# One layer of a four-layer network: a hand-written issue order by slots, with the neighbouring images' stages as pieces in it

## Chip, cores, metric

The kernel runs on one core of one Trainium2 chip. The metric is the device time of one execution in microseconds: the median of the runs, and beside it one profiled execution whose trace all durations come from.

## What is computed

Four layers, each `x = x + layer(group_norm(x))`, on `x` of shape (4 images, 64, 64, 128), all in float32. The change touches layer 0 only, a two-dimensional selective scan:

```python
xz = x @ in_proj_w.T
xh, z = jnp.split(xz, 2, axis=-1)          # 256 channels each
z = jax.nn.silu(z)
xc = silu(depthwise_conv3x3(xh) + conv_b)  # per image 256 x 64 x 64
x0 = xc.reshape(B, 256, L)                 # L = 4096, row by row
x1 = transpose(xc, (0, 1, 3, 2)).reshape(B, 256, L)
xs = stack([x0, x1, x0[..., ::-1], x1[..., ::-1]], axis=1)   # 4 directions
dts, Bm, Cm = split(einsum('bkdl,kcd->bkcl', xs, x_proj_weight), [8, 24], 2)
delta = softplus(einsum('bkrl,kdr->bkdl', dts, dt_projs_weight) + bias)
h[t] = exp(delta[t] * A) * h[t-1] + delta[t] * u[t] * B[t]   # 16 states a channel
y[t] = sum over states of h[t] * C[t]
y = ((y0 + y2[::-1] + transpose(y1 + y3[::-1]) + D * xs) - mean) / sqrt(var + eps)
out = (y * out_norm_w + out_norm_b) * z @ out_proj_w.T
```

## The kernel before

Layer 0 (`layer0`, line 86) runs over the four images one after the other (line 136). Line numbers are those of the listing at the end of this section. For one image:

- **Stage before the scan** (lines 138 to 186). Eight loads of x (`xt`, 512 tokens each), transposes to channels by tokens (line 65), group statistics, one scaling of `xn`. For each half `s` of the 256 channels: the projection `xh` (157), copied into a padded image (158), and the 3x3 convolution as nine matmuls with diagonal weights (163), through Silu into `xc` (170), which stays in SBUF. The gate `z` goes to DRAM (186).
- **Scan** (lines 209 to 306). The image's 4096 tokens are cut in 8 chunks of 512; four directions `k`, in the order 1, 3, 0, 2, give 32 *units* (k, c). `view4` reads `xc` in the direction's order by strides. For each unit `inputs` (189) makes `xd` (the 40 rows of time step, B and C), stores the B rows to DRAM (`bd`), makes `delta` by Softplus and `du = delta * u`. The 16 states go in 4 groups `g` of 4 (`q`). For each state: GpSimd multiplies `dB = du * Bb` (242), where `Bb` is loaded from DRAM to all partitions, ScalarE makes `dA = exp(delta * A)` (245) in PSUM for each half, VectorE runs the scan into `h` (246). In this text one state, so one dB, two dA and two scans, is a *slot*; a unit has 16.
- **Product with C** (lines 253 to 285). For each group `cr` spreads C over partitions (254) and `W` masks it (256). Then for each quarter of the chunk and each half-quarter `e`: four transposes of `h` into PSUM (`pt`, 269), one copy to SBUF (`hT`, 271), and the products `yT` (277), each into 32 of the 128 partitions. A float32 matmul is two records in the trace, a transpose is one.
- **Sum over directions** (287 to 306): `yT` plus what the earlier directions left in DRAM (`yr`), stored again; for k = 2 the layer-norm statistics.
- **Stage after the scan** (309 to 340): normalise, multiply by two broadcast rows and z on GpSimd (322 to 324), transpose (329), output projection (336), add x, store.

Nothing in the file orders this by hand. The framework sorts the instructions of every engine, SyncE's DMA queue included, by its own priorities and places the waits; each engine then runs its list in order. Buffers bound how far engines run apart: `dA`, `pt` and the shared tag `m` (projections, `cr`, convolution) have two PSUM banks each, `dB` and `Bb` three buffers, `h` two, shared with the padded image.

The listing shows the functions touched and their callers.

Of the kernel before, what the change touches and what calls it, by code (L numbers as in the profile page):

```python
# [15 lines left out]
P = 128  # L16
NB = 4
# [7 lines left out]


def view4(t, k, c):

    v = t.rearrange("p s (h w) -> p s h w", w=64)
    if k % 2:  # L30
        v = t.rearrange("p s (h w) -> p s w h", w=64)
    if k < 2:
        return v[:, :, 8 * c : 8 * c + 8, :]
    return v[:, :, 56 - 8 * c : 64 - 8 * c, :][:, :, ::-1, ::-1]


class Shared:
# [19 lines left out]
    def group_norm(self, src, psum, small, keep=None, tag="gt"):  # L57
# [4 lines left out]
        for c in range(NCH):  # L62
# [4 lines left out]
            if keep is not None:  # L67
                nc.scalar.copy(keep[:, c * CH : (c + 1) * CH], ps)
        mv = small.tile([P, 2], F32, name="gn_mv")
# [16 lines left out]
def layer0(sh, A, x_in, x_out, scr):  # L86

    tc, nc = sh.tc, sh.nc  # L90
    with ExitStack() as ctx:
        pool = lambda name, bufs, **kw: ctx.enter_context(tc.tile_pool(name=name, bufs=bufs, **kw))
        wp = pool("l0w", 1)
        big = pool("l0big", 1)
        tmp = pool("l0tmp", 2)
        small = pool("l0small", 2)
        io = pool("l0io", 3)
# [5 lines left out]
        cols = wp.tile([P, 36], F32, name="cols")  # L103
# [5 lines left out]
        on_rows = wp.tile([P, 2, 2 * P], F32, name="on_rows")  # L109
        nc.sync.dma_start(on_rows, A["l0_rows"].partition_broadcast(P))  # L110
# [23 lines left out]
        tiles4 = lambda ap: ap.rearrange("(q p) d -> p q d", p=P)  # L134

        for b in range(NB):

            xn = big.tile([P, NT], F32, name="xn")
            xt = []
            for c in range(NCH):  # L140
                t = io.tile([P, 4, DM], F32, name="xt")
                nc.sync.dma_start(t, tiles4(x_in(b)[c * CH : (c + 1) * CH, :]))
                xt.append(t)
            s_, o_ = sh.group_norm(lambda j: xt[j // 4][:, j % 4, :], ps, small, keep=xn, tag="m")
            nc.vector.tensor_scalar(xn, xn, s_, o_, ALU.mult, ALU.add)


            xc = big.tile([P, 2, NT], F32, name="xc")
            for s in range(2):
                pad = big.tile([P, 66, 66], F32, name="pad", tag="h", bufs=2)  # L150
                nc.gpsimd.memset(pad[:, 0, :], 0.0)
                nc.gpsimd.memset(pad[:, 65, :], 0.0)
                nc.gpsimd.memset(pad[:, 1:65, 0], 0.0)
                nc.gpsimd.memset(pad[:, 1:65, 65], 0.0)
                for c in range(NCH):
                    pm = ps.tile([P, CH], F32, name="xh", tag="m")
                    nc.tensor.matmul(pm, lhsT=w_in[:, s, :], rhs=xn[:, c * CH : (c + 1) * CH], start=True, stop=True)
                    nc.scalar.copy(pad[:, 1 + 8 * c : 9 + 8 * c, 1:65], pm.rearrange("p (h w) -> p h w", w=64))
                for c in range(NCH):
                    pm = ps.tile([P, CH], F32, name="cv", tag="m")  # L160
                    for t in range(9):
# [4 lines left out]
                            rhs=pad[:, 8 * c + dy : 8 * c + dy + 8, dx : dx + 64],  # L166
# [3 lines left out]
                    nc.scalar.activation(xc[:, s, c * CH : (c + 1) * CH], pm, AF.Silu, bias=conv_b[:, s : s + 1])  # L170

            for c in range(NCH):
                z = tmp.tile([P, 4, 2 * P], F32, name="z")
                for e in range(2):
                    zp = ps.tile([P, 2, 2 * P], F32, name="zp", tag="m")
                    for q in range(2):
                        t0 = c * CH + (2 * e + q) * P
                        nc.tensor.matmul(
                            zp[:, q, :],
                            lhsT=xn[:, t0 : t0 + P],  # L180
                            rhs=w_in[:, 2:4, :].rearrange("p s d -> p (s d)"),
                            start=True,
                            stop=True,
                        )
# [987 lines left out]
```

## Time and profile before

| | us |
|---|---|
| median of 3 runs | 10997.95 (10985.44 to 11008.58) |
| profiled execution: its own time | 10996.99 |
| profiled execution: span, first to last instruction | 10995.2 |
| busy TensorE / VectorE / ScalarE / GpSimd | 9042.7 / 7870.9 / 6496.6 / 5549.4 |
| last store's sum of layer 0 (`xr`, line 339) | 7817.6 |
| scans of image 0 / 1 / 2 / 3, first unit's start | 200.7 / 2151.3 / 4102.2 / 6057.9 |

A span is shorter than the execution's time by what lies ahead of the first and behind the last instruction. Busy time of TensorE is modelled from its instructions' size and contains waiting in the pipeline; where it matters, starts are compared instead. The granted clock is TensorE's share of full speed. The idle time at the end of a group's line is that of its engine just before the group's instructions, with what ended most of it.

### The profile page before, as it was taken

The numbers are of one execution on the slowest core, as the hardware profiler recorded it, in microseconds if no ns is written. First come the engines' busy times: TensorE is split into PE (matmuls) and PEld (weight loads), VectorE is DVE, ScalarE is ACT, GpSimd is POOL, SyncE is SP. The second block draws the span as 40 slices with busy tenths as digits, with TensorE's granted clock in tenths as the row PEclk, the third lists the DMA queues.
The fourth block names the chain that finished last, engine by engine and source line by source line (L and its number), as shares of the span: only waits on it lengthen the run. The fifth ranks groups of instructions, "written<-read, shape, count | busy, mean of one in ns | idle before, by whom it ended". The sixth has DMA issues, their size and how long they took to land.

```text
span 10995.2 us, 136237 instructions
## 1 busy us (share of the span) xinstructions
PE 9042.7 (82%) x48616; PEld 4817.3 (44%) x48616; DVE 7870.9 (72%) x11236; ACT 6496.6 (59%) x11794; POOL 5549.4 (50%) x3106
## 2 busy tenths in 40 slices
PE   8888887888888888888887888888797666576777
PEld 4433444443344344334444333444575334344555
DVE  2788887277888717788881778888445876877777
ACT  3778876377888727778871778887222102114555
POOL 2777877277788727778872777887200000000000
PEclk9999999889999988999998899999898667678999
DMA  2223322222233222223322222332300011010000
GB/s 71 86 98 105 108 101 92 74 86 94 101 110 106 86 79 87 95 99 110 105 91 69 97 95 102 107 108 95 106 16 22 20 31 31 0 31 7 9 9 9
DMA packets 375737, 811.01 MB, mean 74 GB/s; under 512 B 24546, under 2 KB 289506, under 8 KB 309266
## 3 DMA queue, kind: packets, MB, share of 16 engines
q1 hardware_dynamic: 372946, 799.82, 21.7%
q8 instruction: 385, 6.31, 0.2%
q14 instruction: 294, 2.41, 0.1%
q10 hardware_dynamic: 2112, 2.48, 0.1%
HBM read 680.58 MB, written 121.63 MB: 73 GB/s over the span
## 4 chain that ended last, share of the span: by engine, by line
PE 61%; DVE 21%; ACT 10%; issue 4%; DMA 2%; POOL 2%; ACTq 0%; DVEq 0%; SPq 0%; POOLq 0%
PE yT L277 15%; PE pt L269 14%; DVE h L246 10%; ACT hT L271 6%; PE cr L254 5%; PE cv L163 5%; PE pm L776 2%; PE xd_ps L193 2%; PE po L923 2%; ACT dA L245 2%; PE dp L201 2%; PE ps L891 1%; DVE W L256 1%; PE po L441 1%; PE pf L436 1%
## 5 line engine op out<-in xcount | busy, mean ns | idle before, releaser
L246 DVE TENSOR_TENSOR_SCAN h<-dA,state,dB 128x512 f32<-128x512 f32 x4096 | 5016.9, 1271 | 1398.9 <-POOL dB L242 699.8
L242 POOL TENSOR_TENSOR dB<-du,Bb 128x1024 f32<-128x1024 f32 x2048 | 4842.1, 2370 | 1267.6 <-DVE h L246 1006.4
L245 ACT ACTIVATE dA<-delta,A_neg 128x512 f32<-128x512 f32 x4096 | 2788.5, 696 | 527.8 <-DVE h L246 514.3
L269 PE MATMUL pt<-ident,h 128*128 128x128 f32 x16384 | 2667.0, 292 | 348.4 <-DVE h L246 348.1
L269 PEld LDWEIGHTS pt<-ident,h 128*128 128x128 f32 x16384 | 1838.6, 145 | 2000.1 <-issue 1280.2
L271 ACT COPY hT<-pt 128x512 f32<-128x512 f32 x4096 | 2252.5, 587 | 748.9 <-PE pt L269 737.8
L277 PE MATMUL yT<-hT,W 128*32 128x256 f32 x16384 | 2324.7, 403 | 355.5 <-ACT hT L271 353.2
L277 PEld LDWEIGHTS yT<-hT,W 128*32 128x32 f32 x16384 | 540.0, 109 | 1440.3 <-ACT hT L271 1019.9
L696 POOL COPY XG<-Xs 64x1 f32<-64x1 f32 x4 | 0.7, 180 | 1784.9 <-ACT Xs L667 1784.9
L204 POOL TENSOR_TENSOR du<-delta,xc 128x1024 f32<-128x1024 f32 x128 | 335.0, 2617 | 763.2 <-ACT delta L202 763.2
L254 PE MATMUL cr<-xd,sel 40*128 40x512 f32 x1024 | 624.6, 715 | 49.4 <-ACT delta L202 36.3
L256 DVE TENSOR_TENSOR W<-cr,diag 128x512 f32<-128x512 f32 x512 | 351.1, 686 | 395.4 <-PE cr L254 264.1
L163 PE MATMUL cv<-pad,taps 128*128 128x512 f32 x1152 | 496.2, 592 | 0.0
L883 POOL COPY vw<-pad 128x196 f32<-128x196 f32 x256 | 76.5, 350 | 702.6 <-PE pv L915 590.7
L193 PE MATMUL xd_ps<-xc,w_x 128*40 128x512 f32 x512 | 354.3, 817 | 93.4 <-DVE W L256 91.1
L776 PE MATMUL pm<-PT,Xs 64*128 64x512 f32 x512 | 380.3, 919 | 16.3 <-DVE pr L777 16.3
L163 PEld LDWEIGHTS cv<-pad,taps 128*128 128x128 f32 x1152 | 216.9, 189 | 278.0 <-issue 274.4
L170 ACT ACTIVATE xc<-cv,cols 128x512 f32<-128x512 f32 x64 | 44.0, 687 | 446.6 <-PE cv L163 446.6
L923 PE MATMUL po<-PT,V 98*128 98x256 f32 x1024 | 278.4, 394 | 35.6 <-DVE PT L919 35.6
L628 ACT COPY S<-pa 128x512 f32<-128x512 f32 x96 | 56.2, 585 | 420.6 <-PE pa L621 420.6
L201 PE MATMUL dp<-xd,w_dt 8*128 8x512 f32 x512 | 291.4, 653 | 6.1 <-ACT xd L195 6.1
L581 PE MATMUL in_pm<-in_mv,tok 128*128 128x32 f32 x48 | 14.1, 386 | 324.4 <-DVE in_mv L579 324.4
(268 smaller groups left out, 9455.2 us busy)
## 6 DMA issues: line engine op xcount, KB each, us to landing
Bb<-l_B SPq DMA_DIRECT2D x512, 1024.0 KB, 4.7
l_y<-y SPq DMA_DIRECT2D x128, 512.0 KB, 3.1
yr<-l_y SPq DMA_DIRECT2D x64, 512.0 KB, 4.8
l_z<-z SPq DMA_DIRECT2D x32, 512.0 KB, 2.9
zf<-l_z SPq DMA_DIRECT2D x32, 512.0 KB, 3.9
yr<-l_y SPq DMA_DIRECT2D x64, 256.0 KB, 4.9
yf<-l_y SPq DMA_DIRECT2D x32, 512.0 KB, 4.7
xt<-in_x SPq DMA_DIRECT2D x32, 256.0 KB, 3.0
```

Source lines behind the costliest of these rows:

```text
L163: nc.tensor.matmul(pm, lhsT=taps[:, s, t, :], rhs=pad[:, 8 * c + dy : 8 * c + dy + 8, dx : dx + 64], start=(t == 0), stop=(t == 8),)
L193: nc.tensor.matmul(xd_ps, lhsT=w_x[:, s, k, :], rhs=u[:, s], start=(s == 0), stop=(s == 1))
L201: nc.tensor.matmul(dp, lhsT=w_dt[:, k, s * P : (s + 1) * P], rhs=xd[0:8, :], start=True, stop=True)
L242: nc.gpsimd.tensor_tensor(dB, du, Bb[:, q : q + 1, :].to_broadcast([P, 2, CH]), ALU.mult)
L245: nc.scalar.activation(dA, delta[:, s, :], AF.Exp, scale=A_neg[:, k, s, n : n + 1])
L246: nc.vector.tensor_tensor_scan(h[:, s, :, q], dA, dB[:, s, :], state[:, s, n : n + 1], ALU.mult, ALU.add)
L254: nc.tensor.matmul(cr, lhsT=sel[:, g, :], rhs=xd, start=True, stop=True)
L269: nc.tensor.transpose(pt[:, r, s, :], h[:, s, t0 : t0 + 32, :].rearrange("p t n -> p (t n)"), sh.ident)
L271: nc.scalar.copy(hT, pt.rearrange("p r s d -> p r (s d)"))
L277: nc.tensor.matmul(yT[e][32 * jo : 32 * jo + 32, qo % 2, :], lhsT=W[:, 4 * q + j, :], rhs=hTs[j // 2][:, j % 2, :], start=((e, jo) not in ...
L776: nc.tensor.matmul(pm, lhsT=Xs[:, r, :], rhs=PT[:, 8 * g : 8 * g + 8, :], start=True, stop=True)
L923: nc.tensor.matmul(po[:, e], lhsT=V[:, half, :], rhs=PT[:, half].rearrange("p h q -> p (h q)"), start=(half == 0), stop=(half == 1),)
```

## The change

The new `layer0` writes the order of TensorE, ScalarE, VectorE and GpSimd itself: everything in the `manual_schedule` block is issued on these four in the order of the program text. SyncE is not in that list and is still ordered by the framework.

- All 128 units of the four images form one loop, 16 slots each. A slot issues dB, its two exp and scan pairs, then one call of `transposed`: the eight transposes and two copies of one quarter of the *oldest finished group*, and behind them the four products of the quarter transposed *one slot earlier*. `h` and `W` have three buffers.
- `cr` comes in every slot with q = 1, `W` with q = 2, the state copies with q = 2 of the next group (the last one in slot 1 of the next unit). The next unit's `inputs` are cut in five and issued in slots 7, 8, 9, 10 and 13; its `u` is fetched in slot 3.
- The stage before the scan is a generator `before(b)`, the stage after it `after(b)`. Image b+1's `before` and image b-1's `after` run beside image b's scan, one piece at most in a slot, in slots 0 to 6 and 13 to 15 if the piece has room (a convolution block needs ten slots in a row, one tap each). What is left at an image's end is issued at once. `before(0)` runs ahead of the block, the last `after` behind the last unit.
- `xc` is no longer kept in SBUF. Each convolution output goes through Silu twice, row by row (`xo`) and transposed (`xw`), and both are stored to DRAM; `fetch` loads a unit's 512 columns from one of them. The stores of `xw` write runs of 8 floats. x is loaded and transposed twice in `before`, once for the statistics and once per chunk with its two neighbouring rows for the convolution (a row projected in two chunks where they overlap).
- The two row products of the layer norm on GpSimd become scale and bias of the copy that follows the transposes on ScalarE. `z` is kept by channels. The D term's products move from direction 2 to direction 0. The sum over directions is added in place in `y`.

The diff, cut to the added lines that matter; the removed ones are in the listing above.

```diff
+        def before(b):
...
+                t = tmp.tile([P, 6, DM], F32, name="xt", bufs=1)
+                nc.sync.dma_start(t[:, 0 : j1 - j0], tiles(x_in(b)[j0 * P : j1 * P, :]))
...
+                for s in range(2):
+                    yield 10
                     pm = ps.tile([P, CH], F32, name="cv", tag="m")
                     for t in range(9):
...
+                        if t < 8:
+                            yield 1
+                    zp = ps.tile([P, CH], F32, name="zp", tag="m")
+                    nc.tensor.matmul(zp, lhsT=w_in[:, 2 + s, :], rhs=xn[:, o : o + CH], start=True, stop=True)
+                    xo = tmp.tile([P, CH], F32, name="xo", tag="t2", bufs=4)
+                    nc.scalar.activation(xo, pm, AF.Silu, bias=conv_b[:, s : s + 1])
+                    nc.sync.dma_start(scr(f"xr{b % 2}")[s, :, c * CH : (c + 1) * CH], xo)
+                    xw = tmp.tile([P, 64, 8], F32, name="xw", tag="t2", bufs=4)
+                    nc.scalar.activation(
+                        xw, pm.rearrange("p (h w) -> p w h", w=64), AF.Silu, bias=conv_b[:, s : s + 1]
+                    )
+                    nc.sync.dma_start(scr(f"xw{b % 2}")[s].rearrange("p (w h) -> p w h", h=64)[:, :, 8 * c : 8 * c + 8], xw)
+                    z = tmp.tile([P, CH], F32, name="z", tag="t2", bufs=4)
+                    nc.scalar.activation(z, zp, AF.Silu)
+                    nc.sync.dma_start(scr(f"z{b % 2}")[s, :, c * CH : (c + 1) * CH], z)
+                    yield 1
...
+                    nc.scalar.activation(yg[:, s, :], pt, AF.Identity, scale=on_w[:, s : s + 1], bias=on_b[:, s : s + 1])
+                    yield 1
...
+                nc.gpsimd.tensor_tensor(yg, yg, z, ALU.mult)
+                yield 2
...
+        def fetch(b, k, c):
+            u = tmp.tile([P, 2, CH], F32, name="u")
+            pc = NCH - 1 - c if k >= 2 else c
+            nc.sync.dma_start(
+                u, scr(f"xw{b % 2}" if k % 2 else f"xr{b % 2}")[:, :, pc * CH : (pc + 1) * CH].rearrange("s p t -> p s t")
+            )
+            return u, (u[:, :, ::-1] if k >= 2 else u)
+        def inputs(k, c, u):
...
+            bd = scr(f"B{(NCH * k + c) % 3}")
+            nc.sync.dma_start(bd, xd[8:24, :])
+            yield
+            dps = []
+            for s in range(2):
+                dp = ps.tile([P, CH], F32, name="dp", tag="m")
+                nc.tensor.matmul(dp, lhsT=w_dt[:, k, s * P : (s + 1) * P], rhs=xd[0:8, :], start=True, stop=True)
+                dps.append(dp)
+                yield
+            delta = tmp.tile([P, 2, CH], F32, name="delta")
+            for s in range(2):
+                nc.scalar.activation(delta[:, s, :], dps[s], AF.Softplus, bias=dt_b[:, k, s : s + 1])
+            yield
+            du = tmp.tile([P, 2, CH], F32, name="du")
+            nc.gpsimd.tensor_tensor(du, delta, u, ALU.mult)
+            yield xd, bd, delta, du
+        for _ in before(0):
+            pass
...
+        def transposed(G):
+            nonlocal copied
+            todo, copied = copied, None
+            if G is not None:
+                q = G["q"]
+                G["q"] += 1
+                pts = []
+                for e in range(2):
+                    pt = ps.tile([P, 2, 2, P], F32, name="pt")
+                    for r in range(2):
+                        t0 = q * P + (2 * e + r) * 32
+                        for s in range(2):
+                            nc.tensor.transpose(
+                                pt[:, r, s, :], G["h"][:, s, t0 : t0 + 32, :].rearrange("p t n -> p (t n)"), sh.ident
+                            )
+                    pts.append(pt)
+                hTs = []
+                for pt in pts:
+                    hT = tmp.tile([P, 2, 2 * P], F32, name="hT", bufs=4)
+                    nc.scalar.copy(hT, pt.rearrange("p r s d -> p r (s d)"))
+                    hTs.append(hT)
+                copied = G, q, hTs
+            if todo is None:
+                return
+            G, q, hTs = todo
+            U = G["unit"]
+            rev = U["rev"]
...
+                if U["k"] == 0:
...
+            for j in range(4):
+                jo = 3 - j if rev else j
+                nc.tensor.matmul(
+                    U["yT"][e][32 * jo : 32 * jo + 32, qo % 2, :],
+                    lhsT=G["W"][:, 4 * q + j, :],
...
+            if G["g"] == 3 and q % 2:
+                y, k = U["y"], U["k"]
+                ye = y[:, 2 * e : 2 * e + 2, :]
+                if k == 1:
+                    nc.scalar.copy(ye, U["yT"][e])
+                else:
+                    nc.vector.tensor_tensor(ye, ye, U["yT"][e], ALU.add)
...
+        order = {mybir.EngineType.PE, mybir.EngineType.Activation, mybir.EngineType.DVE, mybir.EngineType.Pool}
+        pieces = []
+        ends = {}
+        with tc.manual_schedule(engines=order):
+            for i, (b, k, c) in enumerate(units):
+                if i % per == 0:
+                    ln_st = small.tile([P, NJ, 1, 6], F32, name="ln_st")
+                    if b + 1 < NB:
+                        pieces.append([before(b + 1), 1])
...
+                for n in range(NS):
+                    g, q = divmod(n, 4)
+                    if q == 0:
+                        Bb = tmp.tile([P, 4, CH], F32, name="Bb", bufs=3)
+                        nc.sync.dma_start(Bb, bd[4 * g : 4 * g + 4, :].partition_broadcast(P))
+                        h = tmp.tile([P, 2, CH, 4], F32, name="h", bufs=3)
+                        G = dict(unit=unit, g=g, h=h, q=0)
+                    dB = tmp.tile([P, 2, CH], F32, name="dB", bufs=3)
+                    nc.gpsimd.tensor_tensor(dB, du, Bb[:, q : q + 1, :].to_broadcast([P, 2, CH]), ALU.mult)
+                    for s in range(2):
+                        dA = ps.tile([P, CH], F32, name="dA")
+                        nc.scalar.activation(dA, delta[:, s, :], AF.Exp, scale=A_neg[:, k, s, n : n + 1])
+                        nc.vector.tensor_tensor_scan(
+                            h[:, s, :, q], dA, dB[:, s, :], state[:, s, n : n + 1], ALU.mult, ALU.add
+                        )
+                    if n == 1:
+                        for f in ends.pop("state", []):
+                            f()
+                    N = NS * i + n
+                    if N >= 5:
+                        H = queue[0]
+                        transposed(H)
+                        if H["q"] == 4:
+                            queue.pop(0)
+                    if q == 1:
+                        cr = ps.tile([P, CH], F32, name="cr", tag="m")
+                        nc.tensor.matmul(cr, lhsT=sel[:, g, :], rhs=xd, start=True, stop=True)
+                    if q == 2:
+                        W = tmp.tile([P, 16, 32], F32, name="W", bufs=3)
...
+                        G["W"] = W
+                    if q == 3:
+                        queue.append(G)
+                    if c < NCH - 1 and q == 2 and g > 0:
+                        nc.gpsimd.tensor_copy(state[:, :, 4 * g - 4 : 4 * g], last[:, :, CH - 1, :])
+                    if q == 3:
+                        last = h
+                        if g == 3 and c < NCH - 1:
+                            ends["state"] = [
+                                lambda st=state, l=h: nc.gpsimd.tensor_copy(st[:, :, 12:16], l[:, :, CH - 1, :])
+                            ]
+                    if i + 1 < len(units):
+                        if n == 3:
+                            u_next, v_next = fetch(*units[i + 1])
+                        if n in (7, 8, 9, 10):
+                            coming = coming or inputs(*units[i + 1][1:], v_next)
+                            next(coming)
+                        if n == 13:
+                            ready = next(coming)
...
+                    room = 7 - n if n < 7 else 23 - n if n >= 13 else 0
+                    if pieces and room >= pieces[0][1]:
+                        need = next(pieces[0][0], None)
+                        if need is None:
+                            pieces.pop(0)
+                        else:
+                            pieces[0][1] = need
+                if i + 1 < len(units):
+                    u = u_next
+                if i % per == per - 1:
+                    rest = [p for p in pieces]
+                    pieces = []
+                    for p, _ in rest:
+                        for _ in p:
+                            pass
+                    pieces.append([late(after(b, ln_st)), 1])
...
+            for p, _ in pieces:
+                for _ in p:
+                    pass
...
+def late(pieces, n=8):
+    for _ in range(n):
+        yield 1
+    yield from pieces
...
-        l0 = {n: dram.tile([NT, 2 * P], F32, name=f"l0_{n}") for n in ("z", "y0", "y1", "y2", "y3")}
-        l0 |= {f"B{n}": dram.tile([NS, CH], F32, name=f"l0_B{n}") for n in range(4)}
+        l0 = {n: dram.tile([NT, 2 * P], F32, name=f"l0_{n}") for n in ("y0", "y1", "y2", "y3")}
+        l0 |= {n: dram.tile([2, P, NT], F32, name=f"l0_{n}") for n in ("xr0", "xr1", "xw0", "xw1", "z0", "z1")}
+        l0 |= {f"B{n}": dram.tile([NS, CH], F32, name=f"l0_B{n}") for n in range(3)}
...
```

## The prediction on record

> **What bounds the kernel now.** I read the page's slices first, then the stretches of image 0 cut at the start of the scans of each direction, then the groups, then instruction starts on TensorE.
>
> ```profile
> PE   8888887888888888888887888888797666576777
> DVE  2788887277888717788881778888445876877777
> ACT  3778876377888727778871778887222102114555
> POOL 2777877277788727778872777887200000000000
> ```
>
> Four times VectorE, ScalarE and GpSimd fall together to 1 to 3 tenths while TensorE stays at 7 to 8: the norm and convolution stage between images. After slice 28 layer 0 is over (7820 us) and nothing of the rest is touched.
>
> ```profile
> 2.00:200.70 198.70, 180.52 (x439) 81.94 (x440) 13.63 (x37) 47.72 (x73) 5.38 (x6) 0.98 0.18 57
> 200.70:631.40 430.70, 378.83 (x2111) 173.00 (x2109) 334.18 (x288) 331.71 (x554) 331.55 (x166) 0.89 0.25 91
> 1052.10:1442.90 390.80, 339.33 (x2176) 162.93 (x2176) 343.27 (x306) 332.91 (x553) 324.64 (x166) 0.99 0.33 109
> 1862.10:2151.30 289.20, 229.01 (x700) 120.75 (x700) 43.90 (x69) 61.82 (x97) 62.15 (x32) 0.86 0.24 77
> ```
>
> Columns: stretch, length, busy PE, PEld, DVE, ACT, POOL, granted clock, DMA share, GB/s. Head 200 us; scans of direction 1 (53.8 us for each of 8 units), of direction 0 (48.8); border to the next image 289 us. Per image the 32 units take 1661 us (200.7 to 1862.1), a mean of 51.9. No engine is full in the scan: three are near 80%, so a unit is set by waits among them.
>
> ```profile
> L246 DVE TENSOR_TENSOR_SCAN h<-dA,state,dB 128x512 f32<-128x512 f32 x4096 | 5016.9, 1271 | 1398.9 <-POOL dB L242 699.8
> L242 POOL TENSOR_TENSOR dB<-du,Bb 128x1024 f32<-128x1024 f32 x2048 | 4842.1, 2370 | 1267.6 <-DVE h L246 1006.4
> L245 ACT ACTIVATE dA<-delta,A_neg 128x512 f32<-128x512 f32 x4096 | 2788.5, 696 | 527.8 <-DVE h L246 514.3
> L271 ACT COPY hT<-pt 128x512 f32<-128x512 f32 x4096 | 2252.5, 587 | 748.9 <-PE pt L269 737.8
> ```
>
> Scan waits for dB, dB for scan, copy for transposes: a ring of waits. TensorE is in it because of its order:
>
> ```profile
> 1002.60 0.66 PE L269 MATMUL pt<-ident,h 128*128 128x128 f32 x4
> 1003.19 0.62 PE L277 MATMUL yT<-hT,W 128*32 128x256 f32 x4
> 1003.74 0.66 PE L269 MATMUL pt<-ident,h 128*128 128x128 f32 x4
> ...
> 1511.08 1.09 PE L269 MATMUL pt<-ident,h 128*128 128x128 f32 x8
> 1512.10 0.64 PE L277 MATMUL yT<-hT,W 128*32 128x256 f32 x8
> 1512.67 0.69 PE L254 MATMUL cr<-xd,sel 40*128 40x512 f32 x1
> ```
>
> By starts, half a slot alternating (4 transposes, then 4 product records) takes 1.14 us, so 2.28 a slot; eight and eight take 1.02 + 0.57 = 1.59.
>
> **What the skill says.** "TensorE: Matmul & The Clock Gate", Measured speedup vs the span model: products for different groups of 32 columns run at once, three measured at 2.38 times. The trace agrees: eight yT records leave the array in 0.57 us, four in 0.56. The same page, Part 1, has the clock fall when the array idles; here it is lowest (0.89) right after the dense convolutions, so I give a fuller TensorE no better clock: 0.95 below. "ScalarE: Activation LUTs", What ACT_TABLE_LOAD costs: 1283 ns and a drain, 2.66 us a switch. The trace agrees on 1283, but the next activation starts 1.295 us after the load; I use the trace. "DMA: Bandwidth & Descriptors", Rules for kernel authors: a non-contiguous last dim becomes one descriptor per run; its Specifications want 512 bytes. No transfer of before shows 32-byte writes.
>
> **The change, part by part.** Intervals are start to start in the trace: scan 1.175, W 0.59, dA to hT 0.63, hT to hT 0.48, hT to dA 0.48, dA's own length 0.70, dB 2.31, fp32 matmul of 512 columns 2 x 0.43 = 0.86 at full clock.
>
> *Plain slot.* The dA ring of two buffers gives a loop over two slots: scan 1.27, 0.03, dA to hT 0.63, two hT 0.96, dA 0.70, 0.06, scan 1.18 = 4.84, so 2.42 a slot. VectorE alone wants 2.35, GpSimd 2.31 + 0.15 (state copies), TensorE 1.59. The loop sets it: 16 x 2.42 = 38.7. Added to it per unit: three W at 0.45 (each 0.59 less slack), 1.35, the fourth lying under delta; xd copy queued behind its own matmuls in the same slot, with dA behind it, 1.2; delta with two table loads, 0.60 + 1.295 + 0.585 + 0.70 + 1.295 - 0.48 = 4.0; y adds 0.7. Sum 46.0; 0.5 more for waits I can't place: **46.5**. Ends: 45, and 48.6, the best units now. 128 x 46.5 = 5952. TensorE's unit (25.4 + 3.4 cr + 1.7 xd + 1.7 dp = 32 us against 43 to 45 now) hides under that. The contiguous u halves xd for odd directions (0.857 to 0.43 a record) and shortens du (2.86 to 2.36): both covered. Fetching u is one DMA a unit on SP from slot 3 to use in slot 7, some 10 us for a 3 to 5 us transfer: covered. The D products move from direction 2 to 0, the same eight. GpSimd's copy of the last group's state now waits in slot 1 for the scan of slot 15, with the next dB behind it: it loses its lead of two dB, and regains it at 2.42 - 2.31 a slot and in the bursts, so nothing; without that cover up to 2.3 us a unit, which the 48.6 end takes in.
>
> *Convolution in slots.* A block is one chunk and half of the channels, 48 in three images; 44 lie in slots, 4 are flushed at borders. Nine slots carry one tap each: TensorE 9 x (1.59 + 0.86) + 3 cr + zp = 25.5, at clock 0.95 26.8, against 22.7 of the other engines: +4.1. Then ScalarE waits about 1.75 for the last tap, and does load 1.295, xo 0.63, xw 0.63, z 0.5 and load 1.3: +6.1, less 0.5 buffered. Queued behind are dA and so all scans. 9.7 x 44 = **427** (6.6 with tap lag hidden, 11.2 at clock 0.9).
>
> *Rest of the stage before*, an image: 32 xh copies +0.8 (each waits for its matmul in the same slot, dA behind it), 16 xn +0.7, stats 4, group scale with its round trips and Sqrt loads 7: 48, times 3, **144**. *Stage after*, an image: yf 10, pg 11, GpSimd's one product 8 (the two row products of 2.35 are gone), out product 15, xr 8, aggregates and Sqrt 8: 60, times 3, **180**. Each counts whole as nothing is queued deep enough to hide it; fully hidden they'd be 0.
>
> *Borders.* Counting pieces against the room rule, image 0 finishes its neighbour's conv in its 26th unit; in images 1 and 2 sixteen pieces remain and are flushed behind the last unit: 15 taps, two zp and two silu groups, about 20 us, and then the next fetch of u waits for two xw transfers, about 20 more, with TensorE blocked on xd behind it: **80** for both. The three borders of 289 go.
>
> *xw, the transposed store.* Each is 128 x 64 runs of 32 bytes: 8192 descriptors, 16 an image. Bounds from neighbours: A_neg's 1,024 pieces of 64 bytes came through in 2.17 us, 34 ns per engine and packet; eight xt loads, 4,096 of 512 bytes, in 11.4 us, 44 ns. Below 34 nothing here shows; above, writes shorter than 512 bytes might cost twice 34 = 68. I take 40: 512 x 40 ns = 20.5 us. In a slot nothing waits for xw itself, but bd and then Bb stand behind it on SP and the rings: from silu 4 + 20.5 + 1.8 (z) + 1.5 (bd) + 4.7 (Bb) = 32.5 us, and dB of the next unit wants Bb after about 30: 2.5 x 44 = **110**.
>
> *Head.* Image 0's stage is not overlapped, and is now DMA bound: 16 x (20.5 + 1.8) + 14 (x read again) + 40 (stats, first chunk, first inputs) = **410** against 200. *Tail* as now (7710 to 7820): **105**; its flush has one POOL product of 2.35 us where three were, but no overlap between chunks.
>
> Sum: 5952 + 427 + 144 + 180 + 80 + 110 + 410 + 105 = 7408 against 7820 now, **412 less**. On the profiled execution (span 10995.2, time 10997.0) that gives 10,585; the median shown, 10998, differs by 1.
>
> **Rivals.**
> *Short writes decide* (slower). Place: xw in head and behind it Bb. Each ns per packet above 40 costs 16 x 0.512 in the head and 44 x 0.512 in waits, 30.7 us; 412 is used up at 53 ns. At 68: 860 more, 11,445. For it: no packet of this kind measured, bd and Bb directly behind. Against: 64-byte packets at 34, and the DMA share of 0.3. Chance 0.20.
> *Written order stalls.* In-order ACT and DVE behind a late TensorE keep a unit at 51.7: +666, 11,250. For: TensorE's results are wanted in the slot that makes them. Against: 48.6 with a much fuller TensorE. 0.07.
> *Products don't run four abreast*, 1.11 instead of 0.57 in each tap slot: 44 x 9 x 0.54 = +214, 10,800. Against: the 1512.10 line. 0.10.
> *Bursts are hidden better*: unit 45 and conv 7.2: 192 + 110 = 302 better, 10,285. For: VectorE's intervals sum to 41 of the unit's 46.5 (32 x 1.175 + 4 x 0.59 + y). 0.15.
> My case, 10,400 to 10,800 itself: 0.48.
>
> **Numbers.** 0.2% (22 us) is about what can be told from no change. Faster: 0.48 + 0.15 + 0.09 = 0.72; same 0.03; slower 0.25. The range of 8 in 10 leaves some 0.07 below 10,250 and 0.13 above 11,050.
>
> **What would show it.** The slices should lose their four joint dips, the first growing longer. yT runs of eight; direction-0 units near 46.5 in the last image, whose last 24 units carry no pieces; in conv units a stall of VectorE for dA at the silu; 131,072 packets more of 32 bytes an image, whose pace gives xw's price; Bb named as GpSimd's releaser if the rival holds. Wrong if plain units stay above 49.5 or the head passes 800 us.

## The result, and the profile after

| | before | after |
|---|---|---|
| median | 10991.69 us (10969.79 to 11008.58, 4 runs) | 10991.19 us (10985.36 to 11005.71, 4 runs) |
| profiled span | 10995.2 | 10989.4 |
| first unit's start of images 0 / 1 / 2 / 3 | 200.7 / 2151.3 / 4102.2 / 6057.9 | 229.3 / 2090.3 / 4019.5 / 5953.3 |
| start of layer 0's last sum (`xr`) | 7817.6 | 7797.8 |

The ratio is 1.0003 [0.9982, 1.0024]: no change that can be measured. 412 us less were predicted. Line numbers below are those of the changed kernel: the scan is L397, dB L393, dA L396, transposes L310, `hT` L317, `dp` L276, `delta` L281, `cr` L412, `W` L415.

The page's slices of the kernel after, in the same four rows:

```profile
PE   7887887777887877788787777777697666576777
DVE  2767777777776768777676778878345876877777
ACT  2777777777777777777777778777222102114555
POOL 1766667777676667667666677777000000000000
```

Of the four joint dips the three between the images are gone, as the change means them to be; the first, the head, stays. But the level between them fell too: most of the 8s of before are 7s now. What was idle at the borders is now idle everywhere. The stretches (head, image 0, image 3; columns as in the prediction) say the same:

```profile
2.00:229.30 227.30, 187.90 (x480) 83.03 (x480) 21.06 (x52) 50.36 (x92) 6.18 (x18) 0.94 0.60 103
229.30:2090.30 1861.00, 1473.54 (x9220) 776.91 (x9220) 1362.92 (x1257) 1412.52 (x2328) 1301.60 (x680) 0.86 0.34 108
5953.30:7701.00 1747.70, 1336.71 (x9016) 724.53 (x9016) 1387.86 (x1305) 1343.14 (x2239) 1306.78 (x663) 0.85 0.32 111
```

The head is 229 us, not 410. The granted clock in the scans is 0.86, not 0.95. An image with its neighbours' stages in it takes 1861 to 1934 us from its start to the next one's; before it was 1951 to 1956 with the border. The last image, which has only the stage after image 2 in it, takes 1747 us for 32 units, and those of its units that carry no piece (*plain* units; the last one of each direction is left out) take 52.35 us each where 46.5 was predicted. 128 times the difference is some 750 us, more than the predicted gain. Cut at the starts of the scans, the slots of a plain unit have these mean lengths (us):

```
slot   0    1    2    3    4    5    6    7    8    9    10    11   12   13   14   15
     2.49 2.39 2.93 3.14 2.37 3.15 2.95 2.79 2.39 2.49 12.33 2.37 2.50 2.41 3.24 2.40
```

Fifteen slots are near the prediction or below it: 2.37 to 2.5, 0.55 to 0.85 more where W is (2, 6, 14), 0.75 more where y is added (3, 5), 0.4 for xd (7). Slot 10, with `delta` in it, was predicted at 2.42 + 4.0 = 6.4 and takes 12.3. The waits of the whole run name what is late there (engine, what waits, for what: us in total, times, longest):

```profile
DVE h L397 <- ACT dA L396: 1690.0, 453, 18.6
ACT hT L317 <- PE pt L310: 946.2, 535, 5.6
POOL du L284 <- ACT delta L281: 694.8, 128, 42.3
PEld dp L276 <- DVE W L415: 674.6, 127, 16.3
PE dp L276 <- DVE W L415: 567.2, 127, 15.5
```

The last two are new (before, the weight loads of `dp` waited for `W` 10.0 us in all, 0.2 at most), come once in each unit and are long: TensorE waits 4 to 5 us for `W` before `dp`, the product that feeds `delta`. One such slot on the timeline, without the lines that lie off this path (start, length, engine, instruction, in brackets the idle time before it and its releaser; slot 10 begins at 6523.72, slot 11 at 6536.15):

```profile
6523.72 2.46 DVE L397 TENSOR_TENSOR_SCAN h<-dA,state,dB 128x512 f32<-128x512 f32 x2
6526.10 0.67 DVE L415 TENSOR_TENSOR W<-cr,diag 128x512 f32<-128x512 f32 x1
6526.82 2.07 PE L276 MATMUL dp<-xd,w_dt 8*128 8x512 f32 x2 [3.99 <-DVE W L415]
6528.82 1.97 PE L310 MATMUL pt<-ident,h 128*128 128x128 f32 x8
6530.03 0.58 ACT L317 COPY hT<-pt 128x512 f32<-128x512 f32 x1 [5.64 <-PE pt L310]
6530.88 0.58 ACT L317 COPY hT<-pt 128x512 f32<-128x512 f32 x1 [0.27 <-PE pt L310]
6531.48 1.28 ACT L281 ACT_TABLE_LOAD   x1
6532.78 1.26 ACT L281 ACTIVATE delta<-dp,cols 128x512 f32<-128x512 f32 x2
6534.06 1.28 ACT L396 ACT_TABLE_LOAD   x1
6535.35 1.30 ACT L396 ACTIVATE dA<-delta,A_neg 128x512 f32<-128x512 f32 x2
6536.15 1.28 DVE L397 TENSOR_TENSOR_SCAN h<-dA,state,dB 128x512 f32<-128x512 f32 x1 [9.38 <-ACT dA L396]
```

Read it downwards: on this path each step starts when the one above it is done. Two scans, W, `dp`, transposes, copies, load, `delta`, load, dA, scan: each is cheap, and VectorE stands idle for 9.38 us. The cause is in the order of the text. `cr`, `dp` and `xd_ps` share the tag `m` with two PSUM banks. The first half of `dp` comes in slot 8 and holds one bank until `delta` in slot 10. In slot 9 `cr` is issued ahead of the second half of `dp` and takes the other bank until `W` reads it, in slot 10. So the second `dp`, issued in slot 9, can't start before slot 10's scans are over, for `W` stands behind them on VectorE; and TensorE takes its products in the written order, so slot 10's transposes, which have nothing to do with it, stand behind that `dp`, the copies behind them, and `delta` and dA behind the copies. The array also comes out of this wait slow: the granted clock is 1.00 from 6500 to 6525.2 us, and 0.50 from 6526.8 to 6532.0. The two records of this `dp` take 2.0 us to the next start, where a product of 512 columns in float32 takes 0.86 at full clock; over all units they last 1216 and 1056 ns at the median, those of a unit's first `dp` 692 and 587. "TensorE: Matmul & The Clock Gate" in the Trainium skill, Part 1, has the clock drop after idleness; the trace agrees, and the idleness here was this wait of 4 us.

### The profile page after: what moved, and what is told of

It is laid out like the page before. It is cut to its first block, busy times and chain, and to the rows that moved or that the text cites. A ratio compares the mean times of both kernels' runs of the same rounds, so it can differ in the third digit from the quotient of the medians.

```text
span 10989.4 us, 137651 instructions
## 1 busy us (share of the span) xinstructions
PE 8419.9 (77%) x48800; PEld 4864.4 (44%) x48800; DVE 7822.3 (71%) x11296; ACT 6622.3 (60%) x11988; POOL 5362.8 (49%) x3082
## 5 line engine op out<-in xcount | busy, mean ns | idle before, releaser
L397 DVE TENSOR_TENSOR_SCAN h<-dA,state,dB 128x512 f32<-128x512 f32 x4096 | 4973.0, 1269 | 1898.2 <-ACT dA L396 1690.0
L393 POOL TENSOR_TENSOR dB<-du,Bb 128x1024 f32<-128x1024 f32 x2048 | 4834.7, 2369 | 1260.4 <-DVE h L397 1031.7
L310 PE MATMUL pt<-ident,h 128*128 128x128 f32 x16384 | 2678.1, 316 | 884.6 <-ACT hT L317 879.8
L396 ACT ACTIVATE dA<-delta,A_neg 128x512 f32<-128x512 f32 x4096 | 2808.0, 694 | 659.8 <-DVE h L397 587.5
L310 PEld LDWEIGHTS pt<-ident,h 128*128 128x128 f32 x16384 | 2153.8, 161 | 2213.8 <-ACT hT L317 1744.2
L317 ACT COPY hT<-pt 128x512 f32<-128x512 f32 x4096 | 2198.6, 582 | 952.7 <-PE pt L310 946.2
L344 PE MATMUL yT<-hT,W 128*32 128x256 f32 x16384 | 1499.0, 442 | 2.2 <-DVE y L360 2.2
L276 PE MATMUL dp<-xd,w_dt 8*128 8x512 f32 x512 | 393.6, 858 | 567.9 <-DVE W L415 567.2
L284 POOL TENSOR_TENSOR du<-delta,u 128x1024 f32<-128x1024 f32 x128 | 299.7, 2342 | 694.8 <-ACT delta L281 694.8
L185 PE MATMUL cv<-pad,taps 128*128 128x512 f32 x1152 | 614.3, 637 | 5.9 <-ACT xw L200 5.3
L412 PE MATMUL cr<-xd,sel 40*128 40x512 f32 x1024 | 606.6, 674 | 0.0
L344 PEld LDWEIGHTS yT<-hT,W 128*32 128x32 f32 x16384 | 342.8, 115 | 419.2 <-issue 400.6
L276 PEld LDWEIGHTS dp<-xd,w_dt 8*128 8x128 f32 x512 | 96.1, 233 | 731.0 <-DVE W L415 674.6
L415 DVE TENSOR_TENSOR W<-cr,diag 128x512 f32<-128x512 f32 x512 | 341.0, 666 | 0.0
L412 PEld LDWEIGHTS cr<-xd,sel 40*128 40x128 f32 x1024 | 159.6, 195 | 242.8 <-issue 240.7
L267 PE MATMUL xd_ps<-u,w_x 128*40 128x512 f32 x512 | 253.2, 618 | 13.3 <-DMA u<-l_xw 12.1
```

Source lines behind the costliest of these rows:

```text
L185: nc.tensor.matmul(pm, lhsT=taps[:, s, t, :], rhs=pad[:, s, dy : dy + 8, dx : dx + 64], start=(t == 0), stop=(t == 8),)
L276: nc.tensor.matmul(dp, lhsT=w_dt[:, k, s * P : (s + 1) * P], rhs=xd[0:8, :], start=True, stop=True)
L310: nc.tensor.transpose(pt[:, r, s, :], G["h"][:, s, t0 : t0 + 32, :].rearrange("p t n -> p (t n)"), sh.ident)
L317: nc.scalar.copy(hT, pt.rearrange("p r s d -> p r (s d)"))
L344: nc.tensor.matmul(U["yT"][e][32 * jo : 32 * jo + 32, qo % 2, :], lhsT=G["W"][:, 4 * q + j, :], rhs=hTs[j // 2][:, j % 2, :], start=((e, j ...
L393: nc.gpsimd.tensor_tensor(dB, du, Bb[:, q : q + 1, :].to_broadcast([P, 2, CH]), ALU.mult)
```

## The experiments

**The inputs one slot earlier.** On the kernel after; it undoes nothing, and only moves the second `dp` ahead of `cr`.

```diff
-                        if n in (7, 8, 9, 10):
+                        if n in (6, 7, 8, 9):
```

> The next unit's inputs are issued in slots 6 to 9 instead of 7 to 10, nothing else. Theory (two banks of tag m): in the changed kernel the second dp product of slot 9 finds both m banks taken, by the first dp and by cr of slot 9, and cr is freed only by W of slot 10, so TensorE stands with the transposes of slot 10 behind it and slot 10 lasts 12.3 us instead of some 6.4. With dp in slots 7 and 8 no cr is held, the wait dp on W goes (675 us in the changed kernel), the delta slot falls to 6 to 7 us, a plain unit from 52.4 to about 47, and the time from 10,991 to about 10,290 (128 x 5.5). Rival (the order as such is slow, by in-order waits and a TensorE clock of 0.87): the stall moves to another slot and the time stays within 150 us of 10,991.

10192.47 us (10186.11 to 10199.26), ratio to before 0.9273 [0.9257, 0.9289]: 799 us less than after. Plain units 46.92, with `delta` now in slot 9 at 6.37. The waits of `dp` for `W` are gone; in their place `cr` waits for a bank:

```profile
DVE h L397 <- ACT dA L396: 929.2, 361, 18.1
PEld cr L412 <- ACT delta L281: 479.3, 128, 10.6
PE cr L412 <- ACT delta L281: 414.2, 127, 10.1
```

This wait is some 70% as long and costs next to nothing: behind `cr` stands nothing that `delta` needs. And most of the clock comes back, 0.92 to 0.93, without anything else done for it (image 0 and image 3 of this kernel):

```profile
228.20:1865.30 1637.10, 1380.72 (x9220) 723.76 (x9220) 1357.10 (x1256) 1410.86 (x2328) 1293.02 (x679) 0.93 0.38 123
5315.80:6892.00 1576.20, 1248.01 (x9002) 674.10 (x9003) 1392.10 (x1304) 1341.70 (x2237) 1299.07 (x663) 0.92 0.34 123
```

**`cr` and `W` a slot earlier**, the other way to take them out of the collision.

```diff
-                    if q == 1:
+                    if q == 0:
                         cr = ...
-                    if q == 2:
+                    if q == 1:
                         W = ...
```

> The changed kernel with cr in slots of q = 0 and W in slots of q = 1, one slot earlier each; inputs stay in slots 7 to 10. A second way to take the m-bank conflict away that moves no input and leaves dA in PSUM. Theory (two banks of tag m): the second dp of slot 9 still finds its bank held by cr (of slot 8), but W of slot 9 frees it ahead of the transposes of slot 10: slot 10 falls from 12.3 to 6 to 7 us, slot 9 grows by 1 us at most, time 10,200 to 10,350. Rival (the four inputs are late in slots 7 to 10 whatever holds the banks): slot 10 stays above 10 us, time above 10,800.

10544.99 us, ratio 0.9595 [0.9563, 0.9628]; slot 10 takes 8.01, the plain unit 49.31. The direction is right, the size about 0.6 of what was expected: the wait didn't go, it became shorter.

```profile
PEld dp L276 <- DVE W L415: 327.3, 127, 12.8
PE dp L276 <- DVE W L415: 265.8, 127, 12.4
```

`W` is now in the same slot 9 as the second `dp`, behind that slot's scans on VectorE, so the bank comes free one slot sooner and not at once. I had overlooked that.

**dA in SBUF, four banks for tag `m`**, with the inputs where the change put them: more banks instead of another order.

```diff
-                        dA = ps.tile([P, CH], F32, name="dA")
+                        dA = tmp.tile([P, CH], F32, name="dA")
...
-                dp = ps.tile([P, CH], F32, name="dp", tag="m")
+                dp = ps.tile([P, CH], F32, name="dp", tag="m", bufs=4)
```

> The same conflict taken away without moving any slot: dA (still two buffers) lies in SBUF and the two PSUM banks go to tag m, which has four. Theory (two banks of tag m): dp finds a bank in slot 9, slot 10 falls to about 6.4 us, time about 10,250 to 10,350, if exp and scan cost the same with dA in SBUF. Rival (the delta slot is long because of its two table loads and a slow TensorE): slot 10 stays above 11 us and the time near 10,990.

13318.89 us, ratio 1.2119 [1.2095, 1.2142]. The wait for `W` is gone and slot 10 fell to 6.5, only 2.1 more than its neighbours. But these neighbours take 4.4 now, and the total that I expected was missed by 3000 us. Scan and dB of this kernel:

```profile
L397 DVE TENSOR_TENSOR_SCAN h<-dA,state,dB 128x512 f32<-128x512 f32 x4096 | 8727.4, 2191 | 514.4 <-ACT dA L396 314.9
L393 POOL TENSOR_TENSOR dB<-du,Bb 128x1024 f32<-128x1024 f32 x2048 | 5855.9, 2862 | 2618.5 <-DVE h L397 1855.4
```

A scan with both inputs in SBUF takes 2191 ns on the mean (1250 to 3430), with dA in PSUM 1269 (1250 to 1316); dB takes 2862 where it took 2369. "SBUF — State Buffer" in the Trainium skill, section "SBUF: two separate sides", says that VectorE with two SBUF inputs and GpSimd lock each other out for a whole instruction. The numbers fit: the shortest scan is as short as before, and the longest is near 1.25 + 2.34, its own time and one dB. No run tries this lock by itself. As a test of the bank theory this run counts only by slot 10; the total tells of something else.

**Products in the slot of their transposes**, on the kernel with the inputs earlier: the lag undone.

```diff
-                copied = G, q, hTs
+                todo = G, q, hTs
```

> On top of inputs in slots 6 to 9: the products with C take the quarter transposed in the same slot, not the one before (the lag undone). Theory (the lag keeps TensorE out of the ring): TensorE waits for the second copy, some 1.2 us, inside each slot, so its slot is 1.02 + 1.2 + 0.57 = 2.8 us against 2.42 of the ring: 0.4 x 2048 = 800 us slower than with the lag, about 11,050. Rival (TensorE has so much slack that the lag is worth nothing): within 60 us of the kernel with the lag.

11585.37 us, ratio 1.054 [1.0513, 1.0567]: 1393 us more. The plain unit takes 54.58 instead of 46.92. TensorE now waits for the copies ahead of its products, 1.2 us a slot as expected, which hardly shows in the kernel with the lag:

```profile
PEld yT L344 <- ACT hT L317: 2473.3, 4032, 8.1
```

Of the parts tried here the lag is worth the most, and more than the 800 expected.

**No pieces in slots**, on the same kernel: an image's stages are issued at once in slot 3 of the last unit.

```diff
-                    room = 7 - n if n < 7 else 23 - n if n >= 13 else 0
+                    room = 0
...
+                        if n == 3 and i % per == per - 1:
+                            for p, _ in pieces:
+                                for _ in p:
+                                    pass
+                            pieces = []
```

The stage after an image then reads its sums from DRAM when the following image has overwritten most of them; the work is the same.

> On top of inputs in slots 6 to 9: no piece of the neighbouring images is issued in a slot; all of them are issued at once in slot 3 of an image's last unit, ahead of the fetch for the next image. Theory (a piece costs in its slot nearly what it costs alone, since the ring of scans has no buffer to hide it): the borders come back as some 200 us for a stage before and 110 for a stage after, about 1,000 us in all, while 770 us of piece and border cost leave the slots: about 200 to 250 us slower than with pieces. Rival (pieces are hidden in the slots, as the slices of the page suggest): 700 us or more slower.

10436.91 us, ratio 0.9495 [0.9471, 0.952]: 244 more than with the pieces in slots, as the theory had it. All of the interleaving, which is most of the change's text, is worth 244 of 10,190 us.

**Pieces into every gap**: `before` goes first, and a piece of `after` fills a slot that it leaves (three buffers for z; parts of an image's sums are overwritten before they are read).

```diff
-                    if pieces and room >= pieces[0][1]:
+                    for p in pieces:
+                        if room >= p[1]:
```

> On top of inputs in slots 6 to 9: the stage before of the next image stands ahead of the stage after of the previous one, and a piece of the latter takes a slot that the former can't use; z has three scratch tensors instead of two. Nothing is left to flush at an image's end. Theory (border cost is the flush): the last slots of images 1 and 2 fall from 20.5 to 2.5 us, the following waits too, some 2 x 20 = 40 us, and nothing else moves: 10,150. Rival (pieces in slots cost whole wherever they are, the flush is only moved): within 15 us of 10,192.

10182.44 us (10167.67 to 10191.83), ratio 0.9264 [0.9239, 0.9289]: 10 less than with the inputs earlier, which can't be told from nothing. The two flush slots of 20.5 us are gone, some 36 us, but four more slots with a block's Silu came for them at 6.0 us each: the pieces cost nearly as much in slots as in the flush, as the rival had it.

**No table loads for Silu** (the three Silu become Identity), on the kernel with the inputs earlier.

```diff
-                    nc.scalar.activation(xo, pm, AF.Silu, bias=conv_b[:, s : s + 1])
+                    nc.scalar.activation(xo, pm, AF.Identity, bias=conv_b[:, s : s + 1])
```

> On top of inputs in slots 6 to 9: the three activations of each convolution block are Identity instead of Silu, so that the two table switches of a block go; the Silu itself is left out. Theory (work in a slot is paid whole): a block loses 2 x 1.3 us, slot 5 falls from 8.65 to about 6.0, in all 44 x 2.6 = 115 us, 10,075. Rival (the scans in flight hide a load): under 40 us.

10150.69 us, ratio 0.9237 [0.9205, 0.9269]: 42 less, where 115 were expected. In the trace the slot that ends a convolution block is 4.24 over a plain one instead of 5.96, and 44 times 1.7 is 75. These two runs can't tell 42 from 75. By the trace the loads are less than a third of what such a slot costs.

**`xw` stored contiguously** (the transposition left out), on the same kernel.

```diff
-                    nc.sync.dma_start(scr(f"xw{b % 2}")[s].rearrange("p (w h) -> p w h", h=64)[:, :, 8 * c : 8 * c + 8], xw)
+                    nc.sync.dma_start(scr(f"xw{b % 2}")[s, :, c * CH : (c + 1) * CH], xw.rearrange("p w h -> p (w h)"))
```

> On top of inputs in slots 6 to 9: xw is stored as 512 contiguous floats a partition instead of 64 runs of 8, so its values lie in the wrong order (the transposition of the directions 1 and 3 is left out). Theory (short runs are cheap: 8,192 packets landed within 5 us): head and scan change by less than 20 us, 10,190. Rival (bd and Bb queue behind the short runs, as my prediction had it): waits of GpSimd for Bb, 115 us, shrink by half or more, 10,130 or below.

10175.13 us, ratio 0.9259 [0.9229, 0.9288]: 17 less, and the intervals overlap; 9 us of it lie in the head, 219 instead of 228. GpSimd's waits for `Bb` don't shrink (116.6 us, and 114.5 with the short runs), so the rival fell. 524,288 packets of 32 bytes cost nothing that matters here.

**SyncE in the written order too**, on the kernel with the inputs earlier. It was meant to remove a wait for `Bb` that stands in slot 7 of some last units of a direction.

```diff
-        order = {mybir.EngineType.PE, mybir.EngineType.Activation, mybir.EngineType.DVE, mybir.EngineType.Pool}
+        order = {mybir.EngineType.PE, mybir.EngineType.Activation, mybir.EngineType.DVE, mybir.EngineType.Pool, mybir.EngineType.SP}
```

> SyncE is added to the four engines that run in the written order, on the kernel with the inputs one slot earlier. Theory: in that kernel the framework's order of SyncE puts the B rows' broadcasts (Bb) behind the fetch of u whenever a direction changes in the stage before, and GpSimd waits there about 16 us in slot 7 of the last unit of a direction, 16 times; with Bb in its written place those waits go: 64 to 100 us less, about 10,100 to 10,130. Rival: SyncE now waits in the written order for stores (silu outputs, y), and fetches and Bb that stood ahead of them come later: no gain, or some per cent slower, with Bb as the releaser of GpSimd in many units.

10991.18 us (10976.61 to 11001.52), ratio 0.9998 [0.999, 1.0007]: all of the gain is gone, for a new reason. The plain unit is 51.68, and slot 7 is at 7.03 where it was 2.37, in all units. GpSimd's waits in this run, and those in the run before it with the inputs earlier:

```profile
POOL dB L393 <- DMA Bb<-l_B: 1610.0, 152, 30.6
```

```profile
POOL dB L393 <- DMA Bb<-l_B: 114.5, 12, 16.8
```

The rival was right, and my theory of these waits fell. The store of `y` (slot 5) waits for the last product of the unit before, the store of the next B rows (slot 6) for `xd`, and the broadcast of group 2 stands behind both: SyncE's waits for the sum `y` of VectorE rose from 1188.0 to 3243.5 us, while those for a free `Bb` fell from 2489.4 to 1008.3, which says that it reaches the broadcast late. The 12 waits of the second fence, 9.5 us on the mean and not 16 waits of 16, had to have another cause. Eleven of them stand in the last unit of directions 1, 0 and 2, and none in that of direction 3.

**Four buffers for the B rows**, and **SyncE in order with the broadcasts three slots earlier** (the latter with four buffers too).

```diff
-            bd = scr(f"B{(NCH * k + c) % 3}")
+            bd = scr(f"B{(NCH * k + c) % 4}")
```

> The kernel with the inputs one slot earlier, and four DRAM buffers for the B rows where the change has three (index modulo 4 as before the change). In the traces the wait in slot 7 stands in the last unit of directions 1, 0 and 2 and is missing in that of direction 3. With three buffers these units and the ones that follow have the same index: 15 and 24, 7 and 16, 23 and 8; only 31 and 0 differ. So the store of the next unit's B rows, issued in slot 6, goes into the buffer from which groups 2 and 3 still read, the two broadcasts stand behind it, and they read the next unit's rows. Theory: with four buffers the 11 waits go, 4.8 to 5.7 us each: 55 to 60 us less than 10,192, so about 10,135; the slot-7 values of these units fall to 2.4. Rival: the order of SyncE's queue makes the waits, and nothing changes (10,190).

10131.96 us (10127.74 to 10134.57), ratio 0.9209 [0.9193, 0.9225]: 60 less than with three buffers, as expected. Slot 7 of all last units is at 2.37, and of dB's waits for `Bb` one of 4.1 us is left. So the order of directions, 1, 3, 0, 2, together with the modulus made them; all kernels above with three buffers, the changed one among them, use the following unit's B rows in groups 2 and 3 of these 11 units, and so don't compute the scan as written there. With four buffers every unit reads its own rows, and this is the fastest version of the study.

```diff
+                    if q == 1 and g < 3:
+                        N0 = spread(bd, g + 1)
...
                             ready = next(coming)
+                            N0 = spread(ready[1], 0)
```

> SyncE in the written order, the broadcast of a group's B rows issued three slots before its group begins (group 0 of the next unit in slot 13), and four buffers for the B rows. Theory: in the run with SyncE in order all units lose 4.7 us in slot 7, because the store of y (slot 5) and the store of the next B rows (slot 6) stand ahead of group 2's broadcast (slot 8); issued in slot 5, ahead of both, it is in time, and slot 7 falls back to 2.4: about 10,130, like the four-buffer kernel in the framework's order. Rival: other loads behind waiting stores (the sum over directions, the pieces' loads) hold the units in any case, and it stays above 10,400.

10145.38 us (10138.25 to 10150.95), ratio 0.9222 [0.9202, 0.9242]; slot 7 back at 2.38. The written order of SyncE is as good as the framework's if a broadcast stands ahead of the stores that it would wait behind, and no better.

## Why the prediction failed, step by step

Forecast 10,585, measured 10,991: a gain of 412 us was expected and none came. The range of 10,250 to 11,050 held the time, but at its far end; the prediction's own sign of being wrong, plain units above 49.5, is what the trace shows. The sum by its own terms, for the kernel after and for the one with the inputs earlier; plain units here are medians of the slots times 128, and the excess of all slots over them is put down to the piece that was issued in each:

| term | predicted | after | inputs earlier |
|---|---|---|---|
| head | 410 | 229 | 228 |
| 128 plain units | 5952 (46.5) | 6620 (51.7) | 5899 (46.1) |
| conv blocks (taps, Silu) | 427 | 360 | 293 |
| stages, flushes, waits for Bb, all else | 514 | 492 | 473 |
| tail | 105 | 97 | 96 |

**The step that failed** is "*TensorE's unit (25.4 + 3.4 cr + 1.7 xd + 1.7 dp = 32 us against 43 to 45 now) hides under that*", and with it "*delta with two table loads ... = 4.0*", which takes for granted that `dp` is ready when `delta` is issued. I counted TensorE's busy time and found that it fits, but in a written order its place counts: one of the two `dp`, 0.9 us of work, stood where its bank came free a slot too late. That one term was 5.9 us a unit too small, 750 us in all, and moving the inputs by one slot gave 799 back. All that was needed to see it stood in the change: two banks for tag `m`, `cr` at q = 1, `inputs` behind `cr` in slots 7 to 10, `W` at q = 2.

**The rival "written order stalls"** described it, in-order ScalarE and VectorE behind a late TensorE and a unit kept at 51.7; measured are 52.35. What makes TensorE late, the bank, it didn't name. It had a chance of 0.07 because I argued against it with TensorE's share of busy time, the same error. Its 11,250 is above the result mostly because the head came out 181 cheaper and the conv blocks 67.

**Mis-sized terms.** *xw*: 40 ns per engine and packet was assumed, with 34 as the lower bound. In the packet records of one store 8,192 packets pass in 4.94 us, 512 on each engine: 9.65 ns. With it the head is 229 instead of 410, and not DMA bound (TensorE is busy for 187.9 of its 227.3 us), and no Bb waits came from it; the rival "short writes decide" (0.20) was far off. *Conv blocks*: the taps cost 0.1 to 0.3 a slot, not 0.45, and the end 5.8 to 6.0, near the 5.6 predicted. *Plain unit*: the y adds cost 1.5 and not 0.7, xd 0.4 and not 1.2, which nearly cancel. *Bb waits*: 110 predicted, and the eleven slots with these waits are some 100 us longer, but from the shared buffer, which I hadn't seen; that agreement is chance. *Clock*: 0.95 assumed, 0.86 found and 0.93 with the stall gone. Most of the lost clock was an effect of the stall, not a property of the mix. The reading that it was lowest, 0.89, after the convolutions also passed over the 0.86 of the border in the same table.

**What held.** The scan's loop over two dA banks (2.42 a slot; 2.37 to 2.5 found), W at about 0.55 (0.45 predicted), `delta` with two loads at 4.0 (6.37 less 2.4, once the stall was gone), and the products four abreast: runs of eight yT records as in the forecast, 0.57 us to the next start. The three borders went. With the one collision mended, the forecast of 46.5 a unit is 46.92.

**Where the expected gain went**, then: the 412 us were there, and a further 280 in the head, the blocks and the rest; the plain units, 668 above their forecast, took all but some 20 of it back, and behind layer 0 the traces differ by 14 us the other way.

**Open**: how the 6 us at the end of a conv block divide between table loads and the three activations (42 or 75 us of some 260), and why the normalising of `yf` costs 2.4 us in each of 48 slots. VectorE's instruction there takes 409 ns at the median and up to 2456, some 2.0 us more and nearly one dB (2.37); whether it waits for GpSimd there wasn't tried.

## What to carry to other kernels

When a kernel's issue order is written by hand, don't ask whether an engine's busy time fits, but go through the text once for each buffer tag: who takes a bank in which slot, which instruction frees it, and in which slot that one is issued; an allocation whose releaser is issued in a later slot holds up everything behind it on an in-order queue, however short it is. What that costs depends on what stands behind: the wait of `dp` cost some 750 us, the later one of `cr`, some 70% as long, next to nothing. Look for a new wait by its count: one that comes once per unit (127 times here) points to the order of the text, and moving one line is the test. Scratch buffers chosen by an index modulo a number have to be checked at each jump of the index.

## What the hardware showed unexpectedly

- Stores from SBUF of 32-byte runs passed at 9.65 ns per engine and packet. A store's 0.25 MB went through in 4.94 us, 53 GB/s, where the forecast had 20.5 us. The page's issues (last column: us from issue to landing) have 7.9 us for it, and 2.4 for the contiguous store of the same size:

```profile
l_xr<-xo SPq DMA_DIRECT2D x64, 256.0 KB, 2.4
l_xw<-xw SPq DMA_DIRECT2D x64, 256.0 KB, 7.9
```

- A scan with both inputs in SBUF next to a GpSimd product: 1269 to 2191 ns, and the product 2369 to 2862.
- Waits of TensorE for 4 to 5 us once in 52 us lowered the mean granted clock of the scans from 0.93 to 0.86. The clock records of the kernel after hold 1.0 and 0.5 only; 0.5 was granted in 51 to 96% of the time of slots 10 to 13, and in 19% at most of any other.
- A switch of ScalarE's tables cost 1.295 us from the start of the load to that of the next activation, and the load started 17 ns after the end of the activation before it (medians of 386 loads in the kernel after).
